# A low-rank product moved four matmuls forward, its input loaded in three pieces, its first results evicted singly

## The chip, the cores and the metric

The kernel runs on one core of one Trainium2 chip. The metric is the device time of one execution in microseconds (us); where several runs were made, their median.

A core has five engines that run their own instruction streams in order and wait for one another through semaphores: TensorE (PE in the profile; its weight loads are listed as PEld), VectorE (DVE), ScalarE (ACT), GpSimd (POOL) and SyncE (SP, which here issues nearly all DMA loads and stores). Matmuls write to PSUM, and DVE or ACT move results from there to SBUF; this is called an eviction.

## The reference

For 8 sequences of 256 tokens, each with its own adapter number, a rank-16 product is taken of x, and its result goes through a gated feed-forward layer whose linear inputs are rounded to 8-bit floats:

```python
Bx = einsum('bni,bri->bnr', x, B[adapter_ids])        # rank 16
cond = einsum('bnr,bor->bno', Bx, A[adapter_ids])     # width 1024
gate_out = fake_quant_fp8_linear(cond, gate_w, ...)   # 1024 -> 2752
up_out   = fake_quant_fp8_linear(cond, up_w, ...)
hidden = silu(gate_out) * up_out
out = x + fake_quant_fp8_linear(hidden, down_w, ...)  # 2752 -> 1024
```

`fake_quant_fp8_linear` divides its input by a scale, clips it to +-448, rounds it to float8_e4m3 and multiplies it with weights that are already on that grid.

## The kernel before, in words

All data is transposed: features lie on the 128 partitions, tokens in the columns. The 2048 tokens are four blocks t = 0 to 3 of 512 tokens (two sequences each). The width of 1024 is eight groups k of 128; the inner width of 2752 is 22 chunks c, the last of 64.

For each block the adapter makes `xg[t]`, the 8-bit input of the feed-forward layer, in three steps:

1. **B's product**, `bx = B x`: 64 small matmuls over the eight k, in the order of k (`times_b`, all matmuls go through `multiply`, L525). For block 1 this is `two_times_b_in_parts`. Its result is split on DVE and ACT into `bm` (the value rounded for the matmul) and `rest` (what the rounding left), L597 to L608, each copied to the other half of the partitions by ACT.
2. **A's product**, `c = A bm + A rest`: `times_a_parts`, in two parts of four k each; each part fills four PSUM tiles `c0` to `c3` (two for the first two k, two for the last two; one for each sequence) with 16 matmuls. A itself is first prepared by `split` (L454, L455): its first quarter of columns on DVE (in `block_1`), the second on POOL.
3. **The evictions**, `round_two` (L614 on DVE, L616 on ACT): four instructions for each part, each of 128 x 512 values (two k by 256 tokens), scale and round into `xg`. Tokens of the first sequence go through ACT, of the second through DVE.

Then `gate_up(c, t)` takes chunk c of the gate and up weights times `xg[t]`: eight products into `y0` (gate), then eight into `y1` (up), each a matmul of 128 x 128 by 128 x 512. ACT takes silu of `y0` (L702), DVE multiplies it with `y1` into `hid` (L731). `turns` gives the order of k: `(8,)` is all of gate, then all of up; `(2, 2, 2, 2)` takes two k of gate, the same two of up, and so on, for a block whose `xg` is still being made.

PE's order is written out by hand: all matmuls are held in program order. Block 0 goes first, with chunks 0 to 4. In the last of these, `gate_up(4, 0)`, the argument `between={12: block_1}` puts block 1's B product after the twelfth of the sixteen products. Behind the four that are left follow A's product and evictions of block 1, then chunks 0 to 2 of block 1, the adapter of blocks 2 and 3, and everything else. After all chunks comes the down layer, which with the chunks of gate and up makes up nearly the whole time.

The eight PSUM buffers are handed out in turn from one pool (`psum`, tag `ps`); a new tile takes the oldest buffer and waits until the last reader of that buffer is done. SP issues the loads in the order of the code: x of block 0, the adapters of block 0, five chunks of weights (5 MB), then block 1's B, x and A, then x of blocks 2 and 3 and their adapters. The layout of x in HBM follows `PIECES`: for each block the sizes of its pieces in k; each `load_x(t, k)` loads one piece. The framework gives each DMA one of eight semaphores in turn, so an issue also waits for the DMA eight places before it.

Of the kernel before, what the change touches and what calls it, by code (L numbers as in the profile page):

```python
# [21 lines left out]
SEQ = 256  # L22
# [4 lines left out]
NH = H // P  # L27
# [6 lines left out]
NFIRST = 5  # L34
# [2 lines left out]

KS = NH // 2

PIECES = ((2, 3, 2, 1), (7, 1), (NH,), (NH,))  # L40
FP8_MAX = 448.0

SAME_MAX = 240.0
# [17 lines left out]
def x_of(x4, t, k):  # L61

    first = 0
    for n in PIECES[t]:
        if k < first + n:
            break
        first += n
    at = (t * NH + first) * P * TB
    piece = x4[at : at + n * P * TB].rearrange("(p k n) -> p k n", p=P, k=n)
    return piece, first  # L70
# [214 lines left out]
def adaln_ffn(  # L285
# [15 lines left out]
    nc = tc.nc  # L301
# [46 lines left out]
    xg = [kept.tile([P, NH, TB], FP8, name=f"xg{t}") for t in range(2)]  # L348

    with ExitStack() as fast:  # L350
# [26 lines left out]
        def load_b(b, i, adapter, queue):  # L377
            queue.dma_start(
                out=b[:, i * BROW : (i + 1) * BROW], in_=b8[bass.ds(adapter * P, P), :]
            )  # L380
# [9 lines left out]
        def load_a_twice(a, q, src, part):  # L390
            nc.sync.dma_start(
                out=a[32 * q : 32 * (q + 1)], in_=src[bass.ds(part * 2 * R, 2 * R), :]
            )

        def load_x(t, k):
            piece, first = x_of(x4, t, k)
            ks = slice(first, first + piece.shape[1])
            nc.sync.dma_start(out=xs[t][:, ks, :], in_=piece)
# [25 lines left out]
        adapters = [adapter_of(2 + q, nc.sync) for q in range(6)]  # L424
        for j in range(2):
            load_b(b_two[1], j, adapters[j], nc.sync)
        load_x(1, 0)
        for j in range(2):
            adapter = adapters.pop(0)
            for g in range(2):  # L430
                load_a_twice(a_two[1], 2 * g + j, a8_twice, adapter * 2 + g)
        load_x(1, 7)

        for t in (2, 3):
            load_x(t, 0)
# [12 lines left out]
        def split(a, parts, engine):  # L448

            held = tc.keep_in_program_order
            held(engine.tensor_scalar(parts, a, minus, None, ALU.mult))  # L454
            held(engine.tensor_tensor(parts, a, parts.bitcast(F32), ALU.add))  # L455


        def twice(b, n, name, slot):
# [10 lines left out]
        a_parts = [  # L469
            in_place_of_hid(NI - 8 - i, [P, H // 2], F32R, f"a_parts{i}") for i in range(3)  # L470
        ]
# [113 lines left out]
        def two_times_b_in_parts():  # L585

            n = SEQ // 2
            bx = [psum.tile([P, n], F32, tag="ps", name=f"bx{half}") for half in range(2)]  # L590
            times_b([bx[q // 2] for q in range(4)], b_twice[0], n, quads_of_two(1, 0))
            bm = lora.tile([P, 2, n], F32R, name="bm_parts")
            rest = in_place_of_hid(NI - 11, [P, 2, n], F32R, "rest")
            held = tc.keep_in_program_order
            own = [slice(64 * half, 64 * (half + 1)) for half in range(2)]
            for half, copy in enumerate((nc.vector.tensor_copy, nc.scalar.copy)):
                held(copy(bm[own[half], half], bx[half][own[half]]))  # L597
            for half in range(2):
                held(
                    nc.vector.tensor_tensor(  # L600
                        rest[own[half], half],
                        bx[half][own[half]],
                        bm[own[half], half].bitcast(F32),
                        ALU.subtract,
                    )
                )
            for part, half in ((bm, 1), (bm, 0), (rest, 0), (rest, 1)):
                held(nc.scalar.copy(part[own[1 - half], half], part[own[half], half].bitcast(F32)))  # L608
            return [part.rearrange("p h n -> p (h n)") for part in (bm, rest)]

        def round_to(to, c, engine):
            scale = inv[:, GATE_IN : GATE_IN + 1]
            if engine is nc.vector:
                nc.vector.tensor_scalar(to, c, scale, None, ALU.mult, saturate=False)  # L614
            else:
                nc.scalar.activation(to, c, AF.Copy, scale=scale, saturate=False)  # L616

        def round_two(t, part, cs):
            for q in range(4):
                k = KS * part + 2 * (q // 2)  # L620
                to = xg[t][:, k : k + 2, bass.ts(q % 2, SEQ)]
                round_to(to, cs[q], nc.vector if q % 2 else nc.scalar)

        def two_times_a(bm):

# [16 lines left out]
        def times_a_parts(bms, a, at):  # L642

            cs = [psum.tile([P, 2, SEQ], F32, tag="ps", name=f"c{q}") for q in range(4)]
            for bm, i in product(bms, range(2)):
                for q in range(4):
                    rows = slice(32 * q, 32 * (q + 1))
                    multiply(  # L650
                        cs[q][:, i],
                        lhsT=a[rows, bass.ts(at + i, P)],
                        rhs=bm[rows],
                        start=bm is bms[0] and i == 0,
                        stop=bm is bms[-1] and i == 1,
                    )
            return cs

        def two_times_a_parts(bms):
            for part in range(2):  # L660
                round_two(1, part, times_a_parts(bms, a_parts[0], 2 * part))

        def four_times_b():
            quads = [(q, 0, 2 + q // 2, bass.ts(q % 2, SEQ)) for q in range(4)]
# [19 lines left out]
        def gate_up(c, t, turns=(NH,), between={}):  # L684


            tail = c == NI - 1
            w = w_of[c]
            cols = bass.ts(t, TB)
            js = range(1 if tail else 2)  # L690
            ys = []
            steps = []
            for i, n in enumerate(turns):
                done = sum(turns[:i])
                steps += product(js, range(done, done + n))
            rows = slice(TAIL, P) if tail else slice(0, P)
            g = work.tile([P, TB], F32, tag="g", name="g")

            def silu():
                gates = ys[0][:TAIL] if tail else ys[0]  # L700
                early(
                    nc.scalar.activation(  # L702
                        g[rows], gates, AF.Silu, scale=gate_s[: gates.shape[0]]
                    )
                )

            def early(instruction):
                if c < NFIRST:
                    tc.keep_in_program_order(instruction)

            for i, (j, k) in enumerate(steps):
                if i in between:
                    between[i]()
                if j == len(ys):
                    ys.append(psum.tile([P, TB], F32, tag="ps", name=f"y{j}"))
                multiply(
                    ys[j],
                    lhsT=high(w[:, k if tail else k // KS * NH + j * KS + k % KS, :]),
                    rhs=xg[t][:, k, :],
                    start=(k == 0),  # L720
                    stop=(k == NH - 1),
                )
                if j == 0 and k == NH - 1:
                    silu()
            ups = ys[0][TAIL:] if tail else ys[1]
            if tail:
                to = lora.tile([P, 2 * TB], FP8, tag="bm", name="tail", bufs=2)[half_of(t), :TB]
            else:
                to = hid_of(c)[:, cols]
            early(  # L730
                nc.vector.scalar_tensor_tensor(  # L731
                    to,
                    in0=ups,
                    scalar=up_by_down[rows],
                    in1=g[rows],
                    op0=ALU.mult,
                    op1=ALU.mult,
                    saturate=False,
                )
            )  # L740
            if tail:
                nc.vector.tensor_copy(hid_tail[half_of(t), t // 2], to)
            if t == (NTB - 1 if c < NFIRST else 1):
                note_low_bits(w_of[c], P, c)
                if 1 < c <= 1 + 2 * NTB:
                    i, half = divmod(c - 2, 2)
                    ks = slice(half * NH // 2, (half + 1) * NH // 2)
                    note_squares(xg[i][:, ks, :], P, c - 2)
                if c:
                    note_squares(hid[c - 1], P, 2 * NTB + c - 1)  # L750
# [12 lines left out]
        bms = []  # L763

        def block_1():
            split(a_two[1][:, : H // 4], a_parts[0][:, : H // 4], nc.vector)
            bms.append(two_times_b_in_parts())

        gate_up(NFIRST - 1, 0, between={12: block_1})
        two_times_a_parts(bms[0])  # L770
        gate_up(0, 1, turns=(2, 2, 2, 2))
        for c in range(1, NFIRST - 2):
            gate_up(c, 1)
        bms.append(four_times_b())
# [136 lines left out]
    with found_others.Else():  # L911

        k = NH - 1
        cut = TB - P
# [8 lines left out]
        t, cols = NTB - 1, slice(cut, TB)  # L923
# [91 lines left out]
```

## Time and profile before

| | |
|---|---|
| three runs, median (lowest, highest) | 474.89 us (474.71, 474.94) |
| the profiled execution | 474.63 us |
| its span, first to last instruction | 472.8 us |
| PE busy | 468.3 us, 2482 matmuls |
| ACT busy | 193.5 us |
| DVE busy | 106.9 us |
| POOL busy | 11.6 us |
| moved by DMA | 53.84 MB, mean 114 GB/s |

Of the span, 1.8 us of the profiled time lies outside. Busy time of PE contains the latency of matmuls, so that 99% busy does not exclude short stalls. In the page, a slice of the span is 11.8 us; the first three slices show DMA engines 80 to 90% busy and 317 to 421 GB/s, the rest mostly below 150 GB/s. The stage that the change touches lies between 26 and 37 us.

In the listings below, a line of the timeline reads: start, duration, engine, source line, operation, result <- operands, shape, count, and in brackets the idle time ahead of it with what ended it. A line of the chain of waits reads: start, length, what.

### The profile page before, as it was taken

What the parts mean: (1) busy time and instruction counts of PE and PEld (TensorE: products, weight loads), DVE (VectorE), ACT (ScalarE), POOL (GpSimd) and SP (SyncE); (2) the same over time, 40 slices, a digit from 0 to 9 for tenths busy, and PEclk for the clock granted to TensorE, in tenths of its full rate; (3) what the DMA queues carried; (4) which work ended last, traced back from release to release, by engine and by line L of the source; (5) the groups of instructions that cost most, each with busy time, mean ns of one, the idle gap of its engine ahead of it and who ended that gap; (6) DMA issues with size and microseconds to landing.
All of it is one profiled execution on the core that took longest, in us unless ns stands there. A gap on an engine that the chain in (4) does not pass through costs nothing.

```text
span 472.8 us, 5972 instructions
## 1 busy us (share of the span) xinstructions
PE 468.3 (99%) x2482; PEld 215.7 (46%) x2482; DVE 106.9 (23%) x168; ACT 193.5 (41%) x252; POOL 11.6 (2%) x26
## 2 busy tenths in 40 slices
PE   8999999999999999999999999999999999999997
PEld 5454544444444444444444444444444444444444
DVE  1351611212121221212122121231120111031031
ACT  2341548996555655443354544359112022021000
POOL 0023200000000000000000000000000000000000
PEclk9999999999999999999999999999999999999999
DMA  8996024322222201222220021133435345163021
GB/s 317 421 389 200 1 91 143 125 89 89 90 89 90 81 19 79 89 90 89 90 77 21 36 62 57 61 104 103 122 129 161 78 173 162 33 212 107 4 114 69
DMA packets 13909, 53.84 MB, mean 114 GB/s; under 512 B 1650, under 2 KB 2930, under 8 KB 10930
## 3 DMA queue, kind: packets, MB, share of 16 engines
q1 hardware_dynamic: 13664, 53.25, 32.6%
q8 instruction: 21, 0.34, 0.3%
q10 hardware_dynamic: 210, 0.14, 0.1%
q14 instruction: 14, 0.11, 0.1%
HBM read 44.99 MB, written 8.39 MB: 113 GB/s over the span
## 4 chain that ended last, share of the span: by engine, by line
PE 99%; DVE 0%; issue 0%
PE y L525 63%; PE yd L525 32%; PE bx L525 2%; PE warm L525 1%; PE c L525 1%; DVE xg L614 0%; DVE o L822 0%; DVE zeros L312 0%; PE count L525 0%
## 5 line engine op out<-in xcount | busy, mean ns | idle before, releaser
L525 PE MATMUL y<-xg,w_gu 128*128 128x512 fp8e4 x1376 | 298.0, 379 | 0.4 <-DVE xg L614 0.4
L525 PEld LDWEIGHTS <-w_gu 128*128 128x128 bf16 x1376 | 134.2, 98 | 162.5 <-issue 0.6
L525 PE MATMUL yd<-hid,w_d 128*128 128x512 fp8e4 (+2 forms) x693 | 146.0, 373 | 0.0
L702 ACT ACTIVATE g<-y,gate_s 128x512 f32<-128x512 f32 (+1 forms) x88 | 59.7, 682 | 140.9 <-PE y L525 140.9
L731 DVE SCALAR_TENSOR_TENSOR hid<-y,up_by_down,g 128x512 fp8e4<-128x512 f32 x84 | 63.1, 751 | 217.3 <-PE y L525 153.6
L525 PEld LDWEIGHTS <-w_d 128*128 128x128 bf16 x693 | 66.5, 98 | 79.0 <-issue 1.7
L511 ACT ACTIVATE junk<-w_d 128x1408 bf16<-128x1408 uint16 (+1 forms) x16 | 21.2, 1323 | 88.5 <-DMA w_d<-w_d 88.4
L822 DVE SCALAR_TENSOR_TENSOR o<-yd,down_s,x 128x512 f32<-128x512 f32 x28 | 20.0, 748 | 107.3 <-PE yd L525 93.8
L511 ACT ACTIVATE junk<-w_gu 128x2048 bf16<-128x2048 uint16 (+1 forms) x22 | 41.0, 1863 | 0.0
L518 ACT ACTIVATE junk<-hid 128x2048 bf16<-128x2048 fp8e4 x21 | 40.0, 1906 | 0.5
L518 ACT ACTIVATE junk<-xg 128x2048 bf16<-128x2048 fp8e4 x8 | 15.3, 1910 | 0.3
L614 DVE TENSOR_SCALAR xg<-c,inv 128x512 fp8e4<-128x512 f32 x16 | 10.9, 745 | 4.6 <-PE c L525 4.6
L616 ACT ACTIVATE xg<-c,inv 128x512 fp8e4<-128x512 f32 x16 | 9.7, 688 | 1.6 <-PE c L525 1.6
L525 PE MATMUL warm<-zeros 128*128 128x512 bf16 (+1 forms) x27 | 6.9, 418 | 1.2 <-DVE zeros L312 1.2
L822 DVE SCALAR_TENSOR_TENSOR o<-yd,down_s,xg 128x512 f32<-128x512 f32 (+2 forms) x5 | 3.2, 644 | 12.4 <-PE yd L525 9.8
L525 PEld LDWEIGHTS <-zeros 128*128 128x128 bf16 x27 | 2.7, 118 | 5.0 <-issue 3.5
L511 ACT ACTIVATION_READ_ACCUMULATOR junk<-w_gu 128x1 f32 x22 | 4.2, 192 | 0.0
L525 PE MATMUL yd<-hid_tail,w_dt 64*128 64x512 bf16 (+1 forms) x32 | 4.1, 377 | 0.0
L731 DVE SCALAR_TENSOR_TENSOR tail<-y,up_by_down,g 64x512 fp8e4<-64x512 f32 x4 | 3.0, 756 | 4.9 <-ACT g L702 4.8
L518 ACT ACTIVATION_READ_ACCUMULATOR junk<-hid 128x1 f32 x21 | 3.9, 187 | 0.0
L525 PE MATMUL bx<-x,b_four_twice 128*32 128x256 f32 x64 | 3.7, 380 | 0.0
L578 ACT COPY bm<-bx 64x128 f32<-64x128 f32 x2 | 0.5, 262 | 7.1 <-PE bx L525 7.1
(69 smaller groups left out, 55.7 us busy)
## 6 DMA issues: line engine op xcount, KB each, us to landing
w_gu<-w_gu SPq DMA_DIRECT2D x20, 1024.0 KB, 4.8
outT<-o SPq DMA_DIRECT2D x31, 256.0 KB, 2.2
w_d<-w_d SPq DMA_DIRECT2D x8, 704.0 KB, 5.1
w_d<-w_d SPq DMA_DIRECT2D x8, 640.0 KB, 3.9
x<-x SPq DMA_DIRECT2D x2, 2048.0 KB, 12.3
x<-x SPq DMA_DIRECT2D x1, 1792.0 KB, 13.3
w_gu<-w_gu SPq DMA_DIRECT2D x3, 512.0 KB, 4.1
x<-x SPq DMA_DIRECT2D x2, 512.0 KB, 4.0
```

Of the source, the lines that this page charges most:

```text
L511: nc.scalar.activation(junk_like(w), low(w), AF.Copy, accum_out=lows[:rows, column : column + 1])
L518: nc.scalar.activation(junk_like(q), q, AF.Square, accum_out=squares[:rows, column : column + 1])
L525: tc.keep_in_program_order(nc.tensor.matmul(*args, **kwargs))
L578: copy(bm[64 * to : 64 * (to + 1), other], bx[half][64 * half : 64 * (half + 1)],)
L614: nc.vector.tensor_scalar(to, c, scale, None, ALU.mult, saturate=False)
L616: nc.scalar.activation(to, c, AF.Copy, scale=scale, saturate=False)
L702: nc.scalar.activation(g[rows], gates, AF.Silu, scale=gate_s[: gates.shape[0]])
L731: nc.vector.scalar_tensor_tensor(to, in0=ups, scalar=up_by_down[rows], in1=g[rows], op0=ALU.mult, op1=ALU.mult, saturate=False,)
L822: nc.vector.scalar_tensor_tensor(o, in0=y, scalar=down_s, in1=x, op0=ALU.mult, op1=ALU.add)
```

## The change

- `PIECES` cuts block 1's x as 4, 3 and 1 k instead of 7 and 1, and all three loads are issued ahead of the four loads of A; before, the last k came behind A.
- `block_1` is called after the eighth product of chunk 4 (the end of gate) instead of the twelfth, so that eight products of up follow B's product instead of four. Within `block_1`, DVE's `split` of A stands behind B's product with its `bm` and `rest`, before ahead of it.
- In part 0 of block 1, the first two k are evicted one k at a time (128 x 256 values): four instructions, two on each engine, instead of two of 128 x 512; `turns` of the first chunk of block 1 is (1, 1, 2, 2, 2).

```diff
-PIECES = ((2, 3, 2, 1), (7, 1), (NH,), (NH,))
+PIECES = ((2, 3, 2, 1), (4, 3, 1), (NH,), (NH,))
...
-        load_x(1, 0)
+        for k in (0, 4, 7):
+            load_x(1, k)
         for j in range(2):
             adapter = adapters.pop(0)
             for g in range(2):
                 load_a_twice(a_two[1], 2 * g + j, a8_twice, adapter * 2 + g)
-        load_x(1, 7)
...
-        def round_two(t, part, cs):
-            for q in range(4):
-                k = KS * part + 2 * (q // 2)
-                to = xg[t][:, k : k + 2, bass.ts(q % 2, SEQ)]
-                round_to(to, cs[q], nc.vector if q % 2 else nc.scalar)
+        def round_two(t, part, cs, cut=False):
+            for g in range(2):
+                n = 1 if cut and g == 0 else 2
+                for i, j in product(range(0, 2, n), range(2)):
+                    k = KS * part + 2 * g + i
+                    to = xg[t][:, k : k + n, bass.ts(j, SEQ)]
+                    round_to(to, cs[2 * g + j][:, i : i + n], nc.vector if j else nc.scalar)
...
-                round_two(1, part, times_a_parts(bms, a_parts[0], 2 * part))
+                round_two(1, part, times_a_parts(bms, a_parts[0], 2 * part), cut=part == 0)
...
         def block_1():
+            bms.append(two_times_b_in_parts())
             split(a_two[1][:, : H // 4], a_parts[0][:, : H // 4], nc.vector)
-            bms.append(two_times_b_in_parts())
-
-        gate_up(NFIRST - 1, 0, between={12: block_1})
+
+        gate_up(NFIRST - 1, 0, between={8: block_1})
         two_times_a_parts(bms[0])
-        gate_up(0, 1, turns=(2, 2, 2, 2))
+        gate_up(0, 1, turns=(1, 1, 2, 2, 2))
```

## The prediction

> **What bounds the kernel now.** I read the page's chain that ended last first, by engine:
>
> ```profile
> PE 99%; DVE 0%; issue 0%
> ```
>
> Then the waits of TensorE (PE): us in total, times, longest.
>
> ```profile
> PE warm L525 <- DVE zeros L312: 1.2, 1, 1.2
> PE y L525 <- DVE xg L614: 0.4, 1, 0.4
> ```
>
> PE carries the whole chain. Apart from its start it shows one wait, 0.4 us for `xg`, and that one lies in the stage that the change edits. So I took the chain of waits from 26 to 37 us (start, length, what).
>
> ```profile
> 25.90 2.81 PE y L525 x13
> 28.70 0.01 issue
> 28.72 1.95 PE bx L525 x64
> 30.67 0.97 PE y L525 x4
> 31.64 0.57 PE c L525 x7
> 32.22 0.02 issue
> 32.24 0.58 PE c L525 x7
> 32.82 0.75 DVE xg L614
> 33.57 0.05 issue
> 33.62 3.41 PE y L525 x15
> ```
>
> Twelve products of chunk 4, B's product (bx), the last four y, A's product (c) in two parts of 16, one eviction on DVE, then block 1. A matmul's row contains its latency, so the rows of c hide stalls. The timeline shows the starts.
>
> ```profile
> 30.70 0.28 DVE L597 CAST bm_parts<-bx 64x128 fp32r<-64x128 f32 x1
> 31.01 0.61 DVE L600 TENSOR_TENSOR rest<-bx,bm_parts 64x128 fp32r<-64x128 f32 x2
> 31.57 0.44 PEld L525 LDWEIGHTS c<-bm_parts,a_parts 32*128 32x128 f32 x8 [0.42 <-ACT bm_parts L608]
> 31.68 0.75 DVE L731 SCALAR_TENSOR_TENSOR hid<-y,up_by_down,g 128x512 fp8e4<-128x512 f32 x1
> 32.23 0.30 PEld L525 LDWEIGHTS c<-rest,a_parts 32*128 32x128 f32 x8 [0.23 <-ACT rest L608]
> 32.77 1.27 ACT L616 ACTIVATE xg<-c,inv 128x512 fp8e4<-128x512 f32 x2 [0.59 <-PE c L525]
> 32.81 1.41 DVE L614 TENSOR_SCALAR xg<-c,inv 128x512 fp8e4<-128x512 f32 x2 [0.38 <-PE c L525]
> 33.62 0.39 PE L525 MATMUL y<-xg,w_gu 128*128 128x512 fp8e4 x1 [0.39 <-DVE xg L614]
> ```
>
> In the unhindered runs of eight c matmuls (32.58 to 32.81, and from 32.81) the step is 0.0288, so 32 take 0.92. From c's first start, 31.57, to the start of block 1, 33.62, it is 2.05. The stalls are the difference, **1.13 us**: about 0.54 inside c (for the copies of bm and rest, and 0.1 for a PSUM buffer that DVE's L731 frees at 32.43) and 0.58 for the eviction (33.04 to 33.62). That is all this stage can give: 0.24% of the time.
>
> Last, the loads. x's k 0 to 6:
>
> ```profile
> L398 SPq DMA_DIRECT2D x<-x x1: 430/430/430, 15.3 to 15.3; - x1
> DMA to landing us min/median/max: 13.3/13.3/13.3
> ```
>
> They land at 28.55, just before bx at 28.72. Where bx waits for nothing, at 44.08, it starts 0.10 after the slot of the last y (43.12 + 4 x 0.216 = 43.98); here it is 0.18, so bx already loses about 0.08 to this load. The four loads of A land at 28.9 to 29.7 and DVE starts its split of A at 29.76. The last k of x, issued at 23.10, shows no landing; its eight products began near 30.2 with no gap ahead, so it was there.
>
> [...] B at 23.3 and 23.5, x at 28.55, A at 28.9 to 29.7, in order of issue. So I may cut and reorder that stretch of queue by its bytes.
>
> **The change, part by part.**
>
> *B's product earlier.* Four y products, 4 x 0.216 = 0.86, move from before bx to behind it. Without the wait for x, bx would have started at 28.64; it now starts at 27.78.
>
> *x in three.* The same bytes at the same place: k 0 to 3 (1024 of 1792 KB) land near 26.4, since the stretch from B's landing (23.5) takes 5.05 us: 23.5 + 5.05 x 1024/1792. k 4 to 6 land at 28.6, k 7 0.5 to 0.7 later, at 29.1 to 29.3. A load is felt about 0.1 after landing. bx's k 4 is due at 27.78 + 4 x 0.216 = 28.64 (eight matmuls of 0.027), k 7 at 29.29. So x is late by 0.05 to 0.1; I take 0.08 in all, and -0.03 to 0.3 as bounds. bx's last matmul starts at 27.78 + 0.08 + 1.70 = 29.56.
> SP issues one load more. Each of its DMAs waits for the one eight places before, so all later ones hang on the neighbour's landing. Those for A come by about 23.5, ahead of their turn; x of blocks 2 and 3 still queue behind data in flight until 35 and 42, and are used at 44. I cost this at nothing; the cover is over 2 us.
>
> *A last.* B's bytes, x and A together are unchanged, so A ends where k 7 ended: by about 30.2. POOL's half of the split (1.07 + 0.72, and waits) then ends near 32.2, when part 1 of c starts; 0.1 of delay there is hidden under the evictions of part 0.
>
> *The split on DVE goes behind bm and rest.* This is the price. Before, its 0.96 us (29.76 to 30.72) lay under bx. Now DVE does bm and rest first: start 29.56 + 0.28 = 29.84, end 0.92 later at 30.76, then the split until 31.75. c needs it: 31.80. PE is done with eight y at 29.56 + 0.18 + 8 x 0.216 = 31.47, and the switch to c takes 0.09 (31.48 to 31.57 before), so c could start at 31.56: a **new stall of 0.24**. Queued behind the split on DVE is L731 of chunk 4: it starts at 31.75 instead of 31.68, ends at 32.50, and frees the buffer that c's part 1 now takes for its fourth tile. That holds part 1 to about 32.55 and it ends near 32.9.
>
> *The waits inside c's part 0 go.* bm and rest, with their copies, are ready by 31.4: sixteen matmuls run through from 31.80, and the first eviction starts 12 x 0.0288 + 0.42 later, at 32.57 on ACT and 32.61 on DVE (0.42 is from the last matmul on the tile to ACT's start before, 32.35 to 32.77). L731 is out of the way at 32.50.
>
> *Single evictions.* They should let k 0 start after one half. But block 1's y tiles take the PSUM buffers of part 0's first two c tiles, and a buffer comes free only when both its k are evicted. In the changed kernel's instruction order the first product waits for ScalarE's second piece, and the next for VectorE's second. So nothing is gained, and one fixed cost is added on each engine: ACT 32.57 + 0.36 + 0.47 = 33.40, DVE 32.61 + 0.39 + 0.48 = 33.48. The first y starts at 33.40 + 0.06 = 33.46, against 33.42 with whole evictions. Bounds of this edit: a loss of 0.1, or a gain of 0.36 if the buffers didn't bind (then DVE's next whole eviction binds k 2). I take a loss of 0.04. Order 1, 1, 2, 2, 2: k 2 is due at 33.46 + 0.86 = 34.32, its eviction is there at 33.00 + 0.39 + 0.75 + 0.06 = 34.20; later ones follow at 0.66 against 0.86 of products. No further stall.
>
> *Sum.* The same y products are done by 33.46 instead of 33.62: **0.16 us less**. What comes next, bx of blocks 2 and 3 at 44.08, has POOL's copies ready at 43.28 and keeps 0.6. The profiled execution took 474.63, its span 472.8; 0.16 off gives 474.47. The median of the runs is 474.89, 0.26 higher; off that, **474.7**.
>
> **Rivals.** 0.2%, 0.95 us, is about what a measurement of this kernel can tell from no change.
> - *The loads cost somewhat more* (x's pieces or A 0.3 to 1.0 late). For it: x is already at its edge, DMA at its full share. Against: same bytes. 0.5 lost net: 475.2, up to 475.7.
> - *More of the stall goes.* Without DVE's late split (0.24), the wait for x (0.08) and with single evictions that help (0.36) it is 0.16 + 0.68 = 0.84: 474.05; a little over 0.95 if every stall went. Against: those waits stand in the instruction order.
> - *Slower: bx starves on x.* PE runs in order, and at k 4 and k 7 nothing can pass bx; each us that x_4-6 or x_7 lands later is a us lost, there and all the way through bm, split and c. It turns to a loss from 0.16 beyond my landings, and passes 0.95 when k 4 to 6 land after 29.7 or k 7 after 30.4. At 1.3 late: 474.7 + 1.3 = 476.0. [...] Against: k 7 had landed by 30.2 before, with A's bytes ahead of it.
>
> **How the numbers follow.** Forecast 0.60 (own range 474.3 to 475.1: x 0.3 late to the single evictions' gain), dearer loads 0.13, more gain 0.16 (0.07 of it past 0.95), starving 0.11. Faster 0.07; same 0.60 + 0.13 + 0.09 = 0.82; slower 0.11. The range takes in the forecast, the dearer loads and half of the larger gain: 474.1 to 475.7.
>
> **What would show it.** bx near 27.8 to 27.9 with gaps below 0.1 at k 4 and 7; c waiting for DVE's `a_parts` (not ACT's bm) near 31.8; part 0 of c with no wait for rest; the first y of block 1 waiting for the second single evictions near 33.45. I am wrong if c starts without waiting for DVE, if the first y starts after one piece, or if PE shows waits for x over 0.3.

## The result, and the profile after

The changed kernel takes 475.56 us (median; 475.35 to 476.67) against 474.93 (474.71 to 476.17) for the kernel before, in 22 runs each: a ratio of 1.0014, 95% interval 1.0007 to 1.002. It is **0.63 us slower**, where a gain of 0.16 us was forecast. Both lie within the 0.2% that the forecast took for no change, but the time moved the other way.

The profiled executions, 475.81 and 474.63, lie 1.2 us apart. The first reading is where that difference lies. The starts and ends below are from the timelines and the span; the 0.16 of the forecast belongs to the second row. (The y products are those of the feed-forward layer; the first one of block 1 ends the stage that was edited.)

| point of the trace (us) | before | after | difference |
|---|---|---|---|
| first y product of block 0 | 12.14 | 12.45 | 0.31 |
| first y product of block 1 | 33.62 | 33.95 | 0.33 |
| end of the last DVE instruction | 470.32 | 470.64 | 0.32 |
| end of the span | 472.8 | 474.0 | 1.2 |

A third of a microsecond is there before the stage that was edited begins, the stage itself adds nothing and gains nothing, and 437 us later, after the last instruction that computes, comes another 0.8. The waits of SP from 460 us to the end show it; first before, then after (us in total, times, longest):

```profile
SPq L1010 <- DMA outT<-o: 0.2, 1, 0.2
```

```profile
SPq L1012 <- DMA outT<-o: 1.0, 1, 1.0
```

Here SP waits for the last store, in the instructions that end the kernel. The reader would look for a slower store, but the last DVE instruction, and with it the store, is as much later as everything else. I come back to this in the experiments.

The chain of waits of the stage, from 26 to 37 us, after:

```profile
23.84 6.99 DMA a<-a_twice
30.83 0.04 DVEq L454
30.86 0.10 issue
30.96 0.30 DVE rest L600
31.26 0.03 issue
31.29 0.43 DVE a_parts L454
31.72 0.02 issue
31.74 0.43 DVE a_parts L455
32.18 0.14 issue
32.31 0.76 PE c L525 x15
33.07 0.84 ACT xg L616 x2
33.91 0.04 issue
33.95 3.18 PE y L525 x14
```

Before, PE stood in this chain up to the end of c. Now DVE stands ahead of c: rest, then the two instructions of the split. The last load of A, at the head of the chain, lands at 30.83, while DVE is still at the first half of rest (30.65 to 30.93), so that it delays nothing. Behind c it is ACT with two instructions, where DVE had one. The waits of PE in the whole execution:

```profile
PE bx L525 <- DMA x<-x: 0.4, 2, 0.2
PE bx L525 <- DMA b<-b: 0.3, 1, 0.3
PE y L525 <- ACT xg L616: 0.2, 1, 0.2
PE c L525 <- DVE a_parts L455: 0.2, 1, 0.2
```

The waits for `b` and, both times, for `x` belong to block 0 at the start of the kernel (before 9.5 us). They set block 0's start in this execution. The other two are the new waits of the change, in the places the prediction gave. In the stage, x holds up only PE's weight load for k 7, at 29.87 (the PEld line with `x<-x` below). The four matmuls behind it start 0.29 after the four ahead, where the usual step is 0.09: a stall of 0.2. From the timeline:

```profile
28.07 2.22 PE L525 MATMUL bx<-x,b_twice 128*32 128x128 f32 x64
...
29.87 0.16 PEld L525 LDWEIGHTS bx<-x,b_twice 128*32 128x32 f32 x8 [0.29 <-DMA x<-x]
...
30.33 0.28 DVE L597 CAST bm_parts<-bx 64x128 fp32r<-64x128 f32 x1 [3.05 <-PE bx L525]
...
31.09 0.93 POOL L454 TENSOR_SCALAR a_parts<-a,minus 128x256 fp32r<-128x256 f32 x1 [6.52 <-DVE rest L600]
...
31.29 0.42 DVE L454 TENSOR_SCALAR a_parts<-a,minus 128x256 fp32r<-128x256 f32 x1
31.74 0.42 DVE L455 TENSOR_TENSOR a_parts<-a,a_parts 128x256 fp32r<-128x256 f32 x1
...
32.31 0.51 PE L525 MATMUL c<-bm_parts,a_parts 32*128 32x256 f32 x8 [0.18 <-DVE a_parts L455]
...
33.95 3.62 PE L525 MATMUL y<-xg,w_gu 128*128 128x512 fp8e4 x16 [0.21 <-ACT xg L616]
```

### The profile page after: what moved, and what is told of

It reads as the page before. It is cut to its first block, busy times and chain, and to the rows that moved or that the text cites. A ratio compares the mean times of both kernels' runs of the same rounds, so it can differ in the third digit from the quotient of the medians.

```text
span 474.0 us, 5974 instructions
## 1 busy us (share of the span) xinstructions
PE 468.0 (99%) x2482; PEld 215.6 (45%) x2482; DVE 106.9 (23%) x169; ACT 193.6 (41%) x253; POOL 11.5 (2%) x26
## 4 chain that ended last, share of the span: by engine, by line
PE 92%; DMA 5%; ACT 0%; ACTq 0%; SPq 0%; DVE 0%; issue 0%; DVEq 0%
PE y L525 59%; PE yd L525 32%; DMA w_gu<-w_gu 3%; DMA a<-a_twice 1%; DMA a<-a 1%; PE c L525 1%; PE bx L525 1%; SPq L408 0%; ACT L310 0%; ACT xg L616 0%; ACTq L385 0%; ACTq L309 0%; ACTq L378 0%; DVE a_parts L455 0%; DVE a_parts L454 0%
## 5 line engine op out<-in xcount | busy, mean ns | idle before, releaser
L614 DVE TENSOR_SCALAR xg<-c,inv 128x512 fp8e4<-128x512 f32 (+1 forms) x17 | 11.0, 712 | 4.4 <-PE c L525 4.3
L616 ACT ACTIVATE xg<-c,inv 128x512 fp8e4<-128x512 f32 (+1 forms) x17 | 9.8, 664 | 2.2 <-PE c L525 2.2
```

## The experiments

Each kernel was timed against the kernel before on the same chip. "Tail" is the span's end minus the end of the last DVE instruction. Medians of before were 474.82 or 474.83 in these runs. Line numbers move by two or four where an edit adds lines above.

| run | median | ratio (95% interval) | tail | last store on semaphore |
|---|---|---|---|---|
| again_before | 474.85 | 1.0003 (0.9995 to 1.0011) | 2.5 | 7 |
| again_after | 475.60 | 1.0017 (1.0011 to 1.0024) | 3.4 | 0 |
| loads_only | 476.28 | 1.0031 (1.0019 to 1.0042) | 3.4 | 0 |
| cut_only | 474.83 | 1.0000 (0.9992 to 1.0009) | 2.5 | 7 |
| before_one_more | 475.72 | 1.0018 (1.0011 to 1.0025) | 3.4 | 0 |
| before_four_more | 475.13 | 1.0009 (0.9998 to 1.0019) | 2.8 | 3 |
| before_eight_more | 474.87 | 1.0000 (0.9991 to 1.0008) | 2.5 | 7 |
| after_eight_more | 474.66 | 0.9995 (0.9987 to 1.0004) | 2.5 | 7 |
| eight_no_cut | 474.60 | 0.9994 (0.9986 to 1.0002) | 2.5 | 7 |
| eight_split_first | 475.66 | 1.0017 (1.0010 to 1.0024) | 2.5 | 7 |
| move_only | 475.39 | 1.0013 (1.0006 to 1.0020) | 2.5 | 7 |
| x_in_two | 475.66 | 1.0017 (1.0010 to 1.0023) | 2.5 | 7 |

### Which parts of the difference are chance

No edit: both kernels once more (again_before, again_after).

> The kernel before, unchanged, for a second trace of it. The changed kernel's trace is 1.2 us longer in its span than the trace of before, and 0.31 of that lies ahead of the stage (the first matmuls of block 0 wait longer for their loads) and 0.8 behind the last matmul. Theory 'chance': both ends vary from execution to execution, so this trace's first bx and its tail (span end minus the last DVE instruction's end, 2.5 before, 3.4 after) may differ by some tenths from the first trace of before; ratio 1.000. Theory 'ends': start and tail are fixed for a program; then this trace has the first bx at 7.06, the restart at 9.15 and the tail 2.5 again, within 0.1.

> The changed kernel, unchanged. Theory 'chance': the start (block 0's second bx at 9.46, before 9.15) and the tail (3.4) move by some tenths, while the stage from the first bx of block 1 to the end of chunk 0 of block 1 repeats within 0.1. Theory 'ends': the start is 0.3 late and the tail 0.8 longer again. The ratio is 1.001 to 1.002 in both.

The second trace of before has its first y product of block 0 at 12.81 instead of 12.14, so the start moves by over half a microsecond on its own, and the 0.31 of the first row above is no more than chance does. (Ahead of block 0 PE runs warm-up matmuls on zeros. Their step halves from 0.43 to 0.22 us at about 5.9 in the first trace of before and at about 4.5 in that of the changed kernel, so that moment varies too. What made the second trace of before start later is not shown.) But the tail was 2.5 again in before and 3.4 again in the changed kernel. So neither theory was right as a whole: the start varies, the tail doesn't. From here on the tail was the main suspect, and one trace of the stage was no longer enough: again_after shows c's wait for the split at 0.8 where the first trace has 0.2. It is the trace of an execution that took 476.26, 0.66 above the median.

### One part of the change alone

loads_only takes the new `PIECES` and the order of loads, nothing else:

```diff
-PIECES = ((2, 3, 2, 1), (7, 1), (NH,), (NH,))
+PIECES = ((2, 3, 2, 1), (4, 3, 1), (NH,), (NH,))
-        load_x(1, 0)
+        for k in (0, 4, 7):
+            load_x(1, k)
...
-        load_x(1, 7)
```

> Before with only the loads changed: x of block 1 in three pieces ahead of A; B's product stays behind twelve products, the split of A ahead of it. Theory 'A late': A lands about 30.8 instead of 29.7, so DVE's split, which stands ahead of bm in DVE's order, starts about 1.1 later than 29.76, bm is delayed from 30.70 to about 31.8, and the stage loses about 1.1: 1.002. Theory 'start': the third piece or the other layout of x shifts the loads of block 0 as well, first matmuls 0.3 late, on top. Theory of the prediction: A lands at 30.2, split ends at 31.2, 0.5 lost: 1.001.

1.46 us are lost, and the tail is 3.4: the tail comes with the loads. The remaining 0.6 are probably A's: its last load lands at 30.27 in this trace, and DVE's split, ahead of bm here, starts at 30.45 instead of 29.76. That is 0.7 later, between the two expectations, and the chain of waits runs from this landing through the split, bm and rest to c. But the trace is of the fastest of the seven executions. Its first y product of block 1 is only 0.40 later than before, and block 0 began 0.40 late too, so it doesn't weigh A against chance.

cut_only takes the single evictions and `turns=(1, 1, 2, 2, 2)`, nothing else.

> Before with only the single evictions and the turns 1, 1, 2, 2, 2. Prediction: the first y of block 1 waits for ACT's second piece, the next for DVE's second: 0.04 to 0.1 lost in the stage, from no change to 1.0002. If the pieces helped: the first y 0.3 earlier after c's end, 0.9993.

Nothing is gained or lost that can be measured. The waits of PE in this trace show what the first y product waits for now:

```profile
PE y L525 <- ACT xg L616: 0.4, 1, 0.4
```

It was DVE's first eviction before, with the same 0.4. In the chain of waits two evictions on ACT stand one behind the other, up to 33.61, and the product follows at 33.65: it waits for the second piece. That the buffers demand this is read from the kernel; another order of buffers was not tried.

### The tail

In the instructions that end the kernel, SP waits for the eight DMA semaphores in the order 0 to 7. A DMA takes the next semaphore in turn, so the number of DMAs decides on which one the last store falls: 7 before, 0 with one DMA more. The row of SP's last eight such waits, in the rows of the line that ends the kernel; before, then after:

```profile
L1010 SPq EVENT_SEMAPHORE  x8: 17/28/28, 470.9 to 471.9; - x8
```

```profile
L1012 SPq EVENT_SEMAPHORE  x8: 17/28/28, 472.3 to 473.1; - x8
```

Before, the row starts at 470.9, while the store is in flight, and its eighth wait, at 471.9, is the one that the store ends. After, the first is the one that the store ends, at 472.3, and the other seven, whose DMAs had all landed by then, still take until 473.1. The test leaves the edited stage alone and adds DMAs in the middle of the kernel, by loading the weights of some chunks in two:

```diff
-            load_gate_up(c)
+            load_gate_up(c, parts=2 if c in SPLIT else 1)
```

`SPLIT` is chunk 8 in before_one_more, 6 to 9 in before_four_more, 6 to 13 in before_eight_more; in after_eight_more it is 6 to 12, which with the change's own DMA makes eight.

> Before with one DMA more, at a place where nobody waits for it: the weights of chunk 8 in two loads. At the end SP waits for the eight DMA semaphores one after the other, 0 to 7. With one DMA more the last store moves from semaphore 7 (waited for last) to semaphore 0 (waited for first), so that the seven other waits, about 0.84 us in a row, come behind its landing and no longer beside it. Theory 'count of DMAs': tail (span end minus the end of the last DVE instruction) 3.36 instead of 2.53, stage unchanged, time 0.83 us longer: 1.0017. Theory 'place' (x cut in three, its layout or its order makes the tail longer): tail 2.5, ratio 1.000.

> Before with four DMAs more (chunks 6 to 9): last store on semaphore 3, so that four of the seven other waits come behind its landing. Theory 'row of waits': tail between 2.53 and 3.36, from 2.8 (four waits of 0.07) to 3.2 (with the 0.39 that one of them shows): 1.0006 to 1.0014. A theory in which any other count than before's costs 0.83: tail 3.36, 1.0018.

> Before with eight DMAs more (the weights of chunks 6 to 13 in two loads each): last store on semaphore 7 again. Theory 'count of DMAs, modulo eight': tail 2.53 and ratio 1.000, so that cutting these loads costs nothing of itself. If each DMA more had its price, up to 8 x 0.1 = 0.8 more: 1.0017.

> The changed kernel with seven DMAs more (the weights of chunks 6 to 12 in two loads each), eight more than before in all, so that the last store is on semaphore 7 again. Theory 'count of DMAs': tail 2.53, and what is left is the stage alone: by the prediction 0.16 us less than before, 0.9997, 474.7; if the stage loses 0.0 to 0.4 as the two traces of the changed kernel show, 1.000 to 1.0008. Theory 'place': tail 3.4, ratio 1.0015 as the changed kernel.

One DMA that nobody waits for costs the kernel before 0.90 us; four cost 0.30, with a tail of 2.8; eight cost nothing. So it is neither the DMA nor its place, but which of the eight semaphores the last store is on. SP's waits of before_one_more repeat the changed kernel's line:

```profile
SPq L1012 <- DMA outT<-o: 1.0, 1, 1.0
```

With seven more DMAs the changed kernel loses its long tail and falls from 475.60 to 474.66, 0.16 below the kernel before. That is the size of the forecast's gain, but the interval, 0.9987 to 1.0004, does not exclude no gain.

### The steps inside the stage

These runs have the short tail, so that their times can be compared with before and with after_eight_more (474.66).

eight_no_cut: as after_eight_more, with whole evictions and the turns of before.

> The changed kernel with seven DMAs more and with whole evictions and the turns 2, 2, 2, 2 as before. Prediction: the single evictions cost 0.04, so this one is 0.04 faster than the run with single evictions (474.66): 0.9995. If the pieces help after all, it is 0.1 to 0.4 slower: 0.9998 to 1.0004.

474.60, 0.06 faster than with single evictions; 0.04 was expected. A difference of 0.06 is below what the intervals resolve, so the sign is not settled. Neither here nor in cut_only does the cut bring a gain that can be measured.

eight_split_first: as after_eight_more, with DVE's split ahead of B's product again.

```diff
         def block_1():
-            bms.append(two_times_b_in_parts())
             split(a_two[1][:, : H // 4], a_parts[0][:, : H // 4], nc.vector)
+            bms.append(two_times_b_in_parts())
```

> The changed kernel with seven DMAs more and DVE's split of A ahead of B's product again. DVE then waits for A (30.2 to 30.8) before it takes bm; split to 31.2 to 31.8, bm 0.3 and rest 0.6 behind it, their copies on ACT 0.6 more: part 0 of c can take rest only from 32.7 to 33.3, 0.5 to 1.0 later than with the split behind: 1.0006 to 1.0016. If the split behind bm and rest were what costs in the change (0.24), this one is faster than 474.66.

1.00 us slower than with the split behind. Its chain shows why:

```profile
30.58 0.36 DVE a_parts L456
30.95 0.02 issue
30.97 0.58 DVE a_parts L457
31.55 0.21 DVE bm_parts L599
31.76 0.02 issue
31.78 0.30 ACT bm_parts L610
32.08 0.01 issue
32.09 0.30 DVE rest L602
32.40 0.02 issue
32.42 0.30 ACT rest L610
32.73 0.04 issue
32.77 0.55 PE c L527 x8
```

With A landing at 30.4, a split ahead of bm delays bm, rest and ACT's copies, one after the other. Behind rest, the split delays c alone. The execution of this trace took 475.17, 0.49 below the median, and its first y product of block 1 is 0.52 later than in after_eight_more (34.20 against 33.68), so the chain accounts for about half of the 1.00; the rest wasn't traced. Moving the split behind was right once A lands late, though it can make a wait of its own.

move_only: only the place of B's product and of the split; loads and evictions as before.

> Before with only the move: B's product behind eight products and DVE's split behind it, the loads as before (x k 0 to 6, A, k 7), whole evictions. The count of DMAs is that of before, so tail 2.53. bx can't start before x lands at about 28.6, so PE waits 0.85 ahead of it; then eight y, split done 2.2 after bx's last start, c about 32.6, first y of block 1 0.65 late: 1.0014. If the move itself gained, 0.9993.

x_in_two: the whole change, but x in two loads (7 and 1) ahead of A.

```diff
-PIECES = ((2, 3, 2, 1), (4, 3, 1), (NH,), (NH,))
+PIECES = ((2, 3, 2, 1), (7, 1), (NH,), (NH,))
-        for k in (0, 4, 7):
+        for k in (0, 7):
```

> The changed kernel with x of block 1 in two loads (7 and 1) ahead of A instead of three: as many DMAs as before, tail 2.53. bx waits for the 7 k until about 28.6: 0.8 of stall at its start in place of 0.1 to 0.4 inside it. Stage 0.4 to 0.7 longer than the changed kernel's, so 0.3 to 0.7 above before: 1.0007 to 1.0015. If cutting x in three brings nothing, the stage is as the changed kernel's and the ratio 1.000.

Both lose, 0.57 and 0.84 us, and both show PE waiting ahead of bx for x: 0.7 in move_only, and in x_in_two

```profile
PE bx L525 <- DMA x<-x: 0.8, 1, 0.8
```

Without the cut of x, B's product can't start at 27.8, and the four y products moved behind it come too late to hide anything. In x_in_two PE also waits 0.4 ahead of c for DVE's split. So the third piece is worth 1.00 us to this change (x_in_two against after_eight_more), and its DMA took 0.9 of that back at the end of the kernel.

A version better than both: eight_no_cut has the lowest median, 474.60, which is 1.0 below the changed kernel and 0.23 below the kernel before; the latter is not clear of no change (0.9994, 0.9986 to 1.0002).

## Why the prediction was wrong, point by point

- **The step that failed** is in "x in three": "SP issues one load more. Each of its DMAs waits for the one eight places before ... I cost this at nothing; the cover is over 2 us." I followed the shifted semaphores through the loads of the stage, where the cover holds, and not to the end of the program, where SP waits for all eight in a fixed order. There the shift costs 0.83 us of tail (0.90 in the medians of before_one_more). The forecast's gain of 0.16 and this loss of 0.83 make a loss of 0.67; 0.63 was measured.
- *The sum of the stage*, 0.16 less: 0.16 with the tail restored (474.66 against 474.82). That the two agree so well is partly luck: the interval includes no gain, and from the first y product of block 0 to that of block 1 the traces show 21.48 before, and 21.50, 21.88 and 21.17 in after, again_after and after_eight_more.
- *B's product at 27.78*: it starts at 28.07 in an execution whose block 0 began 0.31 late, that is 27.76. But in eight_no_cut, where block 0 began at 12.08, it still starts at 28.08, as PE waited for the weights of an earlier chunk.
- *x late by 0.08*: 0.2 in the first trace, at k 7, whose load lands at 29.83; that is within the bounds of -0.03 to 0.3. PE takes k 7 up 0.04 after the landing, and bx in x_in_two and move_only 0.13 and 0.14 after x's, where I took about 0.1. No later work passed the stalled bx: the y products begin at 30.23, behind its last matmul at 30.02. No stall in after_eight_more and again_after, where k 7 lands at 29.4 and 29.3 and PE shows no wait for x.
- *A by 30.2*: it lands at 30.83 in the first trace, at 30.3 and 30.4 in loads_only and eight_split_first. The loads did land in order of issue in the first trace (k 0 to 3 at 26.17, where the bytes gave 26.4; k 4 to 6 at 28.94, where they gave 28.6; k 7 at 29.83; the last of A at 30.83). In the changed kernel A's lateness is hidden, since DVE is busy with rest until 31.1 to 31.3. Why A lands later than the sum of bytes said was not tried.
- *c waits for DVE's split*: seen in both traces of the changed kernel, 0.18 and 0.83, where 0.24 was forecast. In after_eight_more there is none: c starts at 32.05, as soon as PE has done its eight y, and by the prediction's own sign ("if c starts without waiting for DVE") it was wrong there. The split's length was mis-sized: 0.96 was taken from before; it is 0.87 in the first trace, 0.81 in after_eight_more and 1.5 in again_after.
- *The waits in part 0 of c go, single evictions bring nothing, the first y waits for ACT's second piece*: all as forecast, the last with PE's wait named above. For a single eviction the forecast's sums took 0.36 us from start to start on ACT and 0.39 on DVE, 0.47 and 0.48 in length; no trace had shown these then. The first trace of the changed kernel has 0.37 and 0.36 on ACT (33.06, 33.43, 33.79) and 0.40 and 0.39 on DVE (33.09, 33.50, 33.89), each lasting 0.47 to 0.48. A whole one takes 0.57 to 0.59 on ACT and 0.66 on DVE before, so two singles are 0.14 to 0.16 and 0.13 longer than one whole.
- *The rivals*: bx did not starve (0.2 at most), and the loads of the stage were not the loss; no rival of mine lay outside the stage at all.

## What to carry to other kernels

When an edit changes the number of DMAs, follow the shift in the turn of their semaphores to the last instruction of the program, not only to the next few waits: here one more load, in the first 30 us and well hidden, cost 0.83 us after the last store. Compare start, stage and tail of two traces separately before explaining a difference with the edited stage, and look at a second trace of each before trusting a few tenths. Before evicting a piece early, see whether the next step needs the buffer that still holds the other piece: here the first product waited for both.

## What the runs showed of the hardware

- SP's waits on semaphores that were already satisfied took time: in the changed kernel the seven behind the first took 0.8 us (472.3 to 473.1), and no other engine worked beside them there. Most start 0.06 to 0.08 us after the one ahead, one of them 0.39 after. In before_four_more, with four waits behind the store's, the tail is 0.3 longer than before, about as much as four short steps. What makes the long step is not shown.
- The first y products of block 0 start at 12.14 and 12.81 us in two traces of the same kernel. The step of the warm-up matmuls halves, from 0.43 to 0.22 us, at about 5.9 in the first trace of before and at about 4.5 in the first of the changed kernel. What sets that moment is not shown.
- One matmul's row lasts longer than PE needs for it: before, bx's 64 matmuls of block 1 last 0.27 to 0.30 us each and start 0.027 apart on average (28.72 to 30.40).
- The semaphore of x's load of block 1 before (k 0 to 6) is raised sixteen times: thirteen times by 26.64, then at 27.49, 28.27 and 28.58. B's product starts at 28.72, behind the last: a few late ones set the landing. Why they are late is not shown.
- DVE's two instructions of the split took longer beside some of POOL's half, not beside all of it. In again_after:

```profile
30.62 0.93 POOL L454 TENSOR_SCALAR a_parts<-a,minus 128x256 fp32r<-128x256 f32 x1 [6.13 <-DVE bm_parts L597]
...
31.11 0.58 DVE L454 TENSOR_SCALAR a_parts<-a,minus 128x256 fp32r<-128x256 f32 x1
31.63 0.72 POOL L455 TENSOR_TENSOR a_parts<-a,a_parts 128x256 fp32r<-128x256 f32 x1
31.73 0.91 DVE L455 TENSOR_TENSOR a_parts<-a,a_parts 128x256 fp32r<-128x256 f32 x1
```

  The same two take 0.35 and 0.42 in move_only, where POOL has ended before. In the first trace of the changed kernel they take 0.42 each, though POOL's first instruction lies beside them (31.09 to 32.02). In x_in_two the first one starts at 31.69, while POOL's second runs (31.49 to 32.22), takes 0.68 and ends 0.15 after it; in again_after DVE's second starts 0.10 after POOL's second, takes 0.91 and ends 0.29 after it. Why they take longer is not shown. So part of the 0.83 ahead of c in again_after may be POOL's work; that was read off the traces and not tested by moving POOL's half.
